# Two graph layers in one kernel: the first output bias moved from GpSimd to VectorE, loads and first products reordered, and a new order of work in the last slot

## The chip, the cores and the metric

The kernel runs on one core of one Trainium2 chip. The metric is the device time in microseconds (us) of one execution; the median of three runs of the kernel before is 3541.62 us (3541.19 to 3541.74). All numbers are float32.

Engine names are those of the profile: PE is TensorE (PEld its weight loads), DVE is VectorE, ACT is ScalarE, POOL is GpSimd, SP is SyncE, whose queue (SPq) issues all DMAs here.

## The reference, cut to what matters

There are 32 graphs of 512 nodes with 512 features. Layer 0 is attention with eight heads, weighted by the adjacency matrix, with an output projection, a residual and a layer norm. Layer 1 is a graph attention whose logits are a sum of one number per row and one per column.

```python
# layer 0, per graph
q = x @ Wq.T + bq;  k = x @ Wk.T + bk;  v = x @ Wv.T + bv      # 8 heads of 64
logits = q k^T / 8 + log(clip(adj, 1e-8))
out = softmax(logits) @ v
x = layer_norm(x + out @ Wo.T + bo) * gamma + beta
# layer 1, per graph
f = x @ fc_w.T + fc_b
masked = (f @ q_w.T + q_b) + (f @ k_w.T + k_b)^T + (1 - adj) * -1e9
out = softmax(leaky_relu(masked, 0.01)) @ f + x
```

## The kernel before, in words

**Slots.** The work is one stream, ordered by hand. For each graph ("batch") b of 32 there are four slots p, one for each pair of heads. A slot computes four score tiles (`score`, L754, 128 keys x 2 heads x 512 queries), takes their exponential on ScalarE (L759), multiplies them by the clipped adjacency on VectorE (`factors`, L767, from the tile `cT`), adds them up for the softmax's denominator (`sums`, L777 and L780) and multiplies them with v (`values`, L792). Between these, each slot carries pieces of other batches: projections of the next pair or the next batch (`seven_qk`, `seven_v`, seven products of half size in place of eight, with sums of their operands made on VectorE in `differences`, L560 to L563), the output projection of the batch before (`seven_wo`), its layer norm (`stats_units`, `normalise_units`) and the second layer of the batches before (`dots`, `softmax`, `eT`, `z`, `out_units`). The engines take their instructions in the order written; an instruction waits only for what it reads and for buffers to come free.

**Buffers.** PSUM has three pools: `ps_s` (two tiles of two banks: scores), `ps_o` (one bank: attention times v) and `ps_m` (three banks, used in turn by everything else). In SBUF the tiles `xT`, `n`, `yb` and `T` have a single buffer each.

**Head.** All loads are issued on SP, in program order: x of batch 0 in four pieces, then `load_first_constants` (L150: wq in four pieces, bq, wk in four pieces, bk, wv in one), sixteen loads of 64 KB for `cT` (L483, elements of 128 bytes), then the other constants. PE transposes x (L526), makes q and k of the first pair (L303) and two of the four 128-row units of v (`first_v[:2]`); then the slots begin. The other two units run inside slot (0, 0).

**Constants folded on the chip.** `fold_units` gives three functions that the slots of batches 0 and 1 call. `bias` (slot (0, 1)) adds bv times Wo to bo (L237, L238) and makes eight dot products of fc's rows with q_w and k_w (L241). `offset` (slot (0, 2)) makes the second layer's constant row and folds gamma (L247 to L259). `spread` (slot (1, 0)) sums two vectors over the partitions with a product into `ps_parts` (L273), read by a reduction on VectorE (L274), and broadcasts two more with the products `ps_uq` and `ps_uk` (L267, copied by L268).

**The bias of batch 0.** From batch 1 on, the projected output gets its bias by seeding a PSUM bank with it (`seed` in `seven_wo`, L704). For batch 0, `add_bo` (L281) adds it to the tile `n` on GpSimd with twelve adds of 128x256. The call is in `load_again` at the head of slot (1, 1); POOL has nothing else to do and runs it as soon as the bias is there.

**Denominators.** `divide` writes the sums to DRAM and back in another layout, `divided` (L828 to L838) inverts them there and brings them back as `R`, and `scale` (L847) multiplies.

**The last slot.** `last_slot` is written apart, for batch 31 (b) and the second layer of batch 30 (last). In order:

```python
here2[2]()                        # denominators of pair 2 of batch 31, VectorE (L886 to L892)
here3[2]()                        # the same of pair 3
zs = z(last); zs[0]()             # first of four z products (L439), ScalarE copies it to zT (L440)
wos = seven_wo(b, other_banks(b)); run(wos[:3])   # seed, products 1 2, 5 6
...                               # residual of batch 30 (L432, L433), products 3 7 and 4
run(stats_units(S[b], small, b))  # mean and variance of batch 31 (L330, L331)
run(zs[1:])                       # the other three z products
norm[0](); mask(S[b]); run(norm[1:])   # Ln, Exp (L349, L350), factors (L351 to L355), scaled rows (L359)
```

After that come batch 31's dot products (L369), the row of k values through DRAM to all partitions (`k_rows`, L386 and L388), batch 30's output (`out_units`, `pg`, L452, L453), batch 31's second softmax (L408 to L420), its transposes on PE (`pt_e`, L296), four z products, and four output products (`pg`), each followed by an addition on VectorE (L452) and a store of 128 rows (L453). `find_range` (L918 to L935) turns a record of all denominators into a flag: small operations on VectorE, a PE transpose `pf` (L926), a minimum (L927), a second transpose `one` (L931). The flag decides whether a general path is run afterwards; with these inputs it is not.

Of the kernel before, what the change touches and what calls it, by code (L numbers as in the profile page):

```python
# [19 lines left out]
P = 128  # L20
# [10 lines left out]
def kernel(  # L31
# [118 lines left out]
    def load_first_constants():  # L150
        K["wq"] = load_weight(wqT, "wq", 4)
        K["bq"] = load_col(const, bq, "bq")
        K["wk"] = load_weight(wkT, "wk", 4)
        K["bk"] = load_col(const, bk, "bk")
        K["wv"] = load_weight(wvT, "wv")
# [49 lines left out]
    def fold_units(psum, scratch):  # L205
# [57 lines left out]
        def spread():  # L263
            def copy(vector):
                _, _, _, dg, name, _ = vector
                ps = psum.tile([P, D], FP, tag="m", name=f"ps_{name}")
                nc.tensor.matmul(ps, ones, dg, start=True, stop=True)  # L267
                nc.vector.tensor_copy(K[name], ps)  # L268

            ps = psum.tile([P, D], FP, tag="m", name="ps_parts")  # L270
            for i, (_, _, part, _, _, b0) in enumerate(vectors):
                cols = ps[:, ts(i, DC)]
                nc.tensor.matmul(cols, ones, part, start=True, stop=True)  # L273
                nc.vector.tensor_reduce(extra[:, 0:1], cols, AX.X, ALU.add)  # L274
                nc.vector.tensor_add(b0, b0, extra[:, 0:1])
            for vector in vectors:
                copy(vector)
# [3 lines left out]
    def add_bo(n):  # L281
        left, step = (K["bo"][:, ts(h, H)] for h in range(2))
        for c in range(NC):
            nc.gpsimd.tensor_add(n[:, c, :H], n[:, c, :H], left)
            nc.gpsimd.tensor_add(n[:, c, H:], n[:, c, H:], left)
            nc.gpsimd.tensor_add(n[:, c, H:], n[:, c, H:], step)
# [156 lines left out]
    def out_units(s, dst, psum, name):  # L443
        ps = {}

        def mul(c):
            ps[c] = psum.tile([P, D], FP, tag="m", name=f"pg_{name}_{c}")
            product(ps[c], lambda i: s["zT"][:, i, ts(c, P)], lambda i: K["fc"][:, i, :])

        def add(c):  # L450
            o = s["yb"][:, c, :]
            nc.vector.scalar_tensor_tensor(o, ps[c], s["r"][:, c : c + 1], o, ALU.mult, ALU.add)  # L452
            nc.sync.dma_start(out=dst[ts(c, P), :], in_=o)  # L453
        return [(lambda c=c: mul(c), lambda c=c: add(c)) for c in range(NC)]


    def fast(ctx):
# [31 lines left out]
        def load_again(b):  # L489
# [7 lines left out]
            else:  # L497
                add_bo(s["n"])
# [175 lines left out]
        def seven_wo(b, banks):  # L674
# [53 lines left out]
            def unit3():  # L728
                mul(4, ps["a"], False)
                nc.vector.tensor_add(n21, ps["a"], n21)  # L730
# [180 lines left out]
        def find_range():  # L911
# [4 lines left out]
            def over_elements():  # L916
# [7 lines left out]
                nc.vector.tensor_reduce(low[:, 1:2], t, AX.X, ALU.min)  # L924
                pf = ps_m.tile([P, 512], FP, tag="m", name="pf")
# [11 lines left out]
            return over_elements, over_partitions  # L937
# [33 lines left out]
        def slot(b, p):  # L971
# [12 lines left out]
            run(values(b, p - 1) if p > 0 else values(last, 3) if last >= 0 else [])  # L984
# [30 lines left out]
            if p == 0:  # L1015
# [15 lines left out]
                run(units[2:])  # L1031
                if b == 0:
# [63 lines left out]
        def last_slot():  # L1096
# [31 lines left out]
            here2[2]()  # L1128
            here3[2]()
# [3 lines left out]
            wos = seven_wo(b, other_banks(b))  # L1133
            run(wos[:3])
# [9 lines left out]
            run(zs[1:])  # L1144
# [3 lines left out]
            run(norm[1:])  # L1148
            ks, qs = dots(b)
            run(ks)  # L1150
            k_rows(b)
            run(qs)
            outs = out_units(S[last], out[last], ps_m, last)
# [12 lines left out]
            range_steps = find_range()  # L1166
            range_steps[0]()
            zs[1]()
            flag = range_steps[1]()
            run(zs[2:])  # L1170
            run_out(out_units(S[b], out[b], ps_m, b))
# [8 lines left out]
        run(qk(0, 0) + first_v[:2])  # L1180
# [159 lines left out]
```

## Time and profile before

| what | value |
|---|---|
| median of 3 runs | 3541.62 us |
| profiled execution | 3541.68 us, its span 3539.9 us |
| PE busy | 3507.0 us, 99% of the span |
| DVE busy | 2741.2 us, 77% |
| ACT busy | 1305.9 us, 37% |
| POOL busy | 15.9 us, of which the twelve adds of `add_bo` run from 61.77 to 76.9 |
| mean granted clock of PE | 0.997 of full speed |
| HBM traffic | 61 GB/s over the span |

The profiled execution's own time is 1.8 us longer than the span that its trace covers. A line of a timeline reads: start, length (both us from the span's start), engine, line of the kernel, operation, output <- inputs, shapes, number of instructions merged; the bracket gives the idle time of the engine before it and what ended that. A merged row of several instructions gives their busy time from the first start to the last end. A row of the waits gives the total in us, how often, and the longest. The products are of float32 and each `matmul` of the program stands as two MATMUL instructions in the trace (four products of 128x512 make x8).

### The profile page before, as it was taken

What the parts mean: (1) busy time and instruction counts of PE and PEld (TensorE: products, weight loads), DVE (VectorE), ACT (ScalarE), POOL (GpSimd) and SP (SyncE); (2) the same over time, 40 slices, a digit from 0 to 9 for tenths busy, and PEclk for the clock granted to TensorE, in tenths of its full rate; (3) what the DMA queues carried; (4) which work ended last, traced back from release to release, by engine and by line L of the source; (5) the groups of instructions that cost most, each with busy time, mean ns of one, the idle gap of its engine ahead of it and who ended that gap; (6) DMA issues with size and microseconds to landing.
All of it is one profiled execution on the core that took longest, in us unless ns stands there. A gap on an engine that the chain in (4) does not pass through costs nothing.

```text
span 3539.9 us, 38498 instructions
## 1 busy us (share of the span) xinstructions
PE 3507.0 (99%) x13826; PEld 2045.0 (58%) x13826; DVE 2741.2 (77%) x4685; ACT 1305.9 (37%) x2120; POOL 15.9 (0%) x21
## 2 busy tenths in 40 slices
PE   9999999999999999999999999999999999999998
PEld 3555655655556656555556565565555665655554
DVE  6788877788787788777877877777778778787785
ACT  3334333333334343333333343333334333433442
POOL 1000000000000000000000000000000000000000
PEclk9999999999999999999999999999999999999999
DMA  4344233443233442334432334323344333443220
GB/s 113 49 75 87 46 74 65 77 87 58 70 73 62 87 81 52 75 60 81 87 56 68 71 66 87 69 64 75 61 81 87 52 69 68 72 87 63 68 77 28
DMA packets 880367, 250.68 MB, mean 71 GB/s; under 512 B 807212, under 2 KB 807212, under 8 KB 880168
## 3 DMA queue, kind: packets, MB, share of 16 engines
q1 hardware_dynamic: 880168, 248.15, 35.4%
q8 instruction: 110, 1.80, 0.2%
q14 instruction: 89, 0.73, 0.1%
HBM read 181.93 MB, written 34.65 MB: 61 GB/s over the span
## 4 chain that ended last, share of the span: by engine, by line
PE 96%; DVE 3%; DMA 1%; issue 0%; ACT 0%; SPq 0%; DVEq 0%; ACTq 0%
PE f L579 19%; PE sc L754 13%; PE po L792 13%; PE pz L303 12%; PE pg L303 12%; PE pw_a L199 7%; PE pv_a L199 5%; PE pw_c L199 3%; PE pv_b L199 3%; PE pv_c L199 3%; PE pq L579 2%; PE ps L809 2%; PE pw_b L199 2%; DVE at L767 1%; PE pv L303 0%
## 5 line engine op out<-in xcount | busy, mean ns | idle before, releaser
L759 ACT ACTIVATE at<-sc 128x1024 f32<-128x1024 f32 x512 | 496.4, 1021 | 788.7 <-PE sc L754 787.4
L767 DVE SCALAR_TENSOR_TENSOR at<-cT,at 128x1024 f32<-128x1024 f32 x512 | 603.8, 1221 | 173.3 <-ACT at L759 173.1
L754 PE MATMUL sc<-qT,kT 64*128 64x512 f32 x2048 | 508.9, 615 | 0.8 <-DVE qT L603 0.5
L792 PE MATMUL po<-at,v 128*64 128x512 f32 x2048 | 468.0, 599 | 0.0
L303 PE MATMUL pg<-fc,zT 128*128 128x512 f32 x1024 | 445.5, 593 | 0.2 <-DVE yb L452 0.2
L303 PE MATMUL pz<-eT,n 128*128 128x512 f32 x1024 | 445.5, 593 | 0.0
L754 PEld LDWEIGHTS sc<-qT,kT 64*128 64x128 f32 x2048 | 176.3, 186 | 297.1 <-issue 267.8
L303 PEld LDWEIGHTS pg<-fc,zT 128*128 128x128 f32 x1024 | 194.5, 190 | 233.1 <-issue 216.5
L303 PEld LDWEIGHTS pz<-eT,n 128*128 128x128 f32 x1024 | 194.7, 190 | 230.4 <-issue 220.8
L792 PEld LDWEIGHTS po<-at,v 128*64 128x64 f32 x2048 | 135.6, 137 | 316.5 <-issue 312.8
L780 DVE TENSOR_TENSOR as<-as,at 128x1024 f32<-128x1024 f32 x254 | 308.4, 1214 | 5.5
L579 PE MATMUL f<-T,qk_s 128*128 128x256 f32 x992 | 246.4, 381 | 8.5 <-DVE qT L588 4.3
L440 ACT COPY zT<-pz 128x512 f32<-128x512 f32 x128 | 74.9, 585 | 435.4 <-PE pz L303 435.4
L579 PEld LDWEIGHTS f<-T,qk_s 128*128 128x128 f32 x992 | 185.8, 191 | 38.7 <-DVE qT L588 5.1
L579 PE MATMUL f<-xT,wq 128*128 128x256 f32 x744 | 191.8, 380 | 0.0
L800 ACT COPY oT<-po 128x512 f32<-128x512 f32 x128 | 75.1, 587 | 288.1 <-PE po L792 288.1
L777 DVE TENSOR_TENSOR as<-at,at 128x1024 f32<-128x1024 f32 x128 | 154.2, 1204 | 2.2
L579 PEld LDWEIGHTS f<-xT,wq 128*128 128x128 f32 x744 | 139.0, 191 | 22.4
L591 ACT ACTIVATE qT<-f,bq 128x256 f32<-128x256 f32 x124 | 58.7, 473 | 234.9 <-PE f L579 234.9
L579 PE MATMUL f<-xT,qk_s 128*128 128x256 f32 x496 | 128.6, 382 | 0.0
L579 PE MATMUL f<-T,wk 128*128 128x256 f32 x496 | 127.3, 379 | 0.0
L579 PE MATMUL f<-xT,wk 128*128 128x256 f32 x496 | 127.3, 379 | 0.0
(204 smaller groups left out, 4582.6 us busy)
## 6 DMA issues: line engine op xcount, KB each, us to landing
cT<-in_adj_dram SPq DMA_DIRECT2D x512, 64.0 KB
out_dram<-yb SPq DMA_DIRECT2D x128, 256.0 KB
R<-d SPq DMA_DIRECT2D x126, 256.0 KB
x<-in_x_dram SPq DMA_DIRECT2D x124, 256.0 KB
e<-in_adj_dram SPq DMA_DIRECT2D x31, 1024.0 KB
n<-in_x_dram SPq DMA_DIRECT2D x31, 1024.0 KB
eP<-e SPq DMA_DIRECT2D x480, 64.0 KB
w<-dk SPq DMA_DIRECT2D x32, 256.0 KB
```

The lines of the kernel that those rows point to most:

```text
L199: nc.tensor.matmul(to[:, n, :], data(i, c)[:, ts(n, P)], weights[i][:, c, :], start=(first and n == 0 and c == 0), stop=(n == KH - 1 and c ...
L303: nc.tensor.matmul(ps, lhs(i), rhs(i), start=(i == 0), stop=(i == 3))
L440: nc.scalar.copy(s["zT"][:, d, :], pz)
L579: nc.tensor.matmul(to, left[i][:, c, ts(p, P)], s["B"][i][:, c, :], start=(first and c == 0), stop=(c == KH - 1), skip_group_check=True,)
L754: nc.tensor.matmul(sc[:, j, :], s["kT", p][rows, ts(kc, P)], s["qT", p][rows, :], start=True, stop=True,)
L759: nc.scalar.activation(at, sc, AF.Exp, scale=SCALE)
L767: nc.vector.scalar_tensor_tensor(at, cT[:, kc, :].unsqueeze(1).to_broadcast([P, 2, N]), ADJ_MIN, at, ALU.max, ALU.mult,)
L777: nc.vector.tensor_add(s["as", p], s["at", p, 0], s["at", p, 1])
L780: nc.vector.tensor_add(s["as", p], s["as", p], s["at", p, kc])
L792: nc.tensor.matmul(s["po", p][j * DK : (j + 1) * DK, :], s["v"][h // 4][:, kc, ts(h % 4, DK)], s["at", p, kc][:, j, :], start=(kc == 0), s ...
L800: nc.scalar.copy(s["oT"][p], s["po", p])
L809: nc.tensor.matmul(ps[h * BL : (h + 1) * BL, :], ones[:, :BL], s["as", p + h // 2][:, h % 2, :], start=True, stop=True,)
```

## The change

There are six parts.

1. Loads: bq and bk are loaded before wq, and wk is loaded as one DMA of 1 MB instead of four of 256 KB.
2. First products: only the first unit of v runs ahead of slot (0, 0); the second runs between that slot's first and second pair of score tiles.
3. `add_bo` runs on VectorE, with three adds of 128x1024 that broadcast the bias over the four row blocks, called at the end of slot (1, 0).
4. `spread` makes `uq` and `uk` first, and `ps_parts` after them.
5. The last slot: the seeds of `seven_wo` come ahead of pair 3's division and of the first zT copy; product 4 of `seven_wo` goes into a bank of its own and is added apart; the layer norm's operations on ScalarE come after the second z product and so ahead of the zT copies of the third and fourth; `find_range`'s small operations on VectorE come right after the dot products of q, and only its PE part stays among the z products.
6. The last output block is computed, added and stored in two halves of 256 columns.

```diff
--- before.py
+++ after.py
@@ -148,10 +148,10 @@
     K = {}
 
     def load_first_constants():
+        K["bq"] = load_col(const, bq, "bq")
+        K["bk"] = load_col(const, bk, "bk")
         K["wq"] = load_weight(wqT, "wq", 4)
-        K["bq"] = load_col(const, bq, "bq")
-        K["wk"] = load_weight(wkT, "wk", 4)
-        K["bk"] = load_col(const, bk, "bk")
+        K["wk"] = load_weight(wkT, "wk")
         K["wv"] = load_weight(wvT, "wv")
 
     def load_constants():
@@ -267,23 +267,24 @@
                 nc.tensor.matmul(ps, ones, dg, start=True, stop=True)
                 nc.vector.tensor_copy(K[name], ps)
 
+            for vector in vectors:
+                copy(vector)
             ps = psum.tile([P, D], FP, tag="m", name="ps_parts")
             for i, (_, _, part, _, _, b0) in enumerate(vectors):
                 cols = ps[:, ts(i, DC)]
                 nc.tensor.matmul(cols, ones, part, start=True, stop=True)
                 nc.vector.tensor_reduce(extra[:, 0:1], cols, AX.X, ALU.add)
                 nc.vector.tensor_add(b0, b0, extra[:, 0:1])
-            for vector in vectors:
-                copy(vector)
 
         return [bias, offset, spread]
 
     def add_bo(n):
-        left, step = (K["bo"][:, ts(h, H)] for h in range(2))
-        for c in range(NC):
-            nc.gpsimd.tensor_add(n[:, c, :H], n[:, c, :H], left)
-            nc.gpsimd.tensor_add(n[:, c, H:], n[:, c, H:], left)
-            nc.gpsimd.tensor_add(n[:, c, H:], n[:, c, H:], step)
+        left, step = (
+            K["bo"][:, ts(h, H)].unsqueeze(1).to_broadcast([P, NC, H]) for h in range(2)
+        )
+        nc.vector.tensor_add(n[:, :, :H], n[:, :, :H], left)
+        nc.vector.tensor_add(n[:, :, H:], n[:, :, H:], left)
+        nc.vector.tensor_add(n[:, :, H:], n[:, :, H:], step)
 
 
     def transpose_units(src, dst, psum, evict, name):
@@ -440,18 +441,27 @@
             nc.scalar.copy(s["zT"][:, d, :], pz)
         return [lambda d=d: unit(d) for d in range(DC)]
 
-    def out_units(s, dst, psum, name):
+    def out_units(s, dst, psum, name, halve=False):
+
         ps = {}
 
-        def mul(c):
-            ps[c] = psum.tile([P, D], FP, tag="m", name=f"pg_{name}_{c}")
-            product(ps[c], lambda i: s["zT"][:, i, ts(c, P)], lambda i: K["fc"][:, i, :])
-
-        def add(c):
-            o = s["yb"][:, c, :]
-            nc.vector.scalar_tensor_tensor(o, ps[c], s["r"][:, c : c + 1], o, ALU.mult, ALU.add)
-            nc.sync.dma_start(out=dst[ts(c, P), :], in_=o)
-        return [(lambda c=c: mul(c), lambda c=c: add(c)) for c in range(NC)]
+        def mul(c, cols):
+            ps[c, cols.start] = psum.tile(
+                [P, cols.stop - cols.start], FP, tag="m", name=f"pg_{name}_{c}_{cols.start}"
+            )
+            product(ps[c, cols.start], lambda i: s["zT"][:, i, ts(c, P)],
+                    lambda i: K["fc"][:, i, cols])
+
+        def add(c, cols):
+            o = s["yb"][:, c, cols]
+            nc.vector.scalar_tensor_tensor(
+                o, ps[c, cols.start], s["r"][:, c : c + 1], o, ALU.mult, ALU.add
+            )
+            nc.sync.dma_start(out=dst[ts(c, P), cols], in_=o)
+        parts = [(c, slice(0, D)) for c in range(NC)]
+        if halve:
+            parts[-1:] = [(NC - 1, slice(h * H, (h + 1) * H)) for h in range(2)]
+        return [(lambda a=a: mul(*a), lambda a=a: add(*a)) for a in parts]
 
 
     def fast(ctx):
@@ -494,8 +504,6 @@
                 s["n"] = act.tile([P, NC, D], FP, tag="n", name=f"n_{b}")
             if b > 0:
                 load_b(s["n"], x[b])
-            else:
-                add_bo(s["n"])
             if b < B - 1:
                 s["e"] = act.tile([P, NC, N], FP, tag="L1", name=f"e_{b}", bufs=2)
                 load_b(s["e"], adj[b])
@@ -671,7 +679,7 @@
                 nc.vector.tensor_add(c21, ps["a"], c21)
             return [unit0, unit1, unit2, unit3]
 
-        def seven_wo(b, banks):
+        def seven_wo(b, banks, apart=False):
 
 
 
@@ -726,8 +734,13 @@
                 nc.vector.tensor_add(n22, ps["a"], n22)
 
             def unit3():
-                mul(4, ps["a"], False)
-                nc.vector.tensor_add(n21, ps["a"], n21)
+                if apart:
+                    mul(4, ps["b"], True)
+                    nc.vector.tensor_add(n21, ps["a"], n21)
+                    nc.vector.tensor_add(n21, ps["b"], n21)
+                else:
+                    mul(4, ps["a"], False)
+                    nc.vector.tensor_add(n21, ps["a"], n21)
             return [seed, unit0, unit1, unit2, unit3]
 
         def long_banks(b):
@@ -922,6 +935,8 @@
                 nc.vector.tensor_mul(t, t, t)
                 nc.vector.tensor_scalar(t, t, 0.25, None, ALU.is_le)
                 nc.vector.tensor_reduce(low[:, 1:2], t, AX.X, ALU.min)
+
+            def turn():
                 pf = ps_m.tile([P, 512], FP, tag="m", name="pf")
                 nc.tensor.transpose(pf[:2, :P], low, ident)
                 nc.vector.tensor_reduce(least, pf[:2, :P], AX.X, ALU.min)
@@ -934,7 +949,7 @@
                 flag = const.tile([1, 1], I32, name="flag")
                 nc.vector.tensor_scalar(flag, bad, -1.0, 1.0, ALU.mult, ALU.add)
                 return flag
-            return over_elements, over_partitions
+            return over_elements, turn, over_partitions
 
         def work(b):
             S[b]["w"] = io.tile([P, 4, N], FP, tag="x", name=f"w_{b}")
@@ -981,7 +996,7 @@
             if p == 1 and last >= 0:
                 wos = seven_wo(last, long_banks(last))
                 run(wos[:1])
-            run(values(b, p - 1) if p > 0 else values(last, 3) if last >= 0 else [])
+            run(values(b, p - 1) if p > 0 else values(last, 3) if last >= 0 else first_v[1:2])
             if p == 0 and last >= 0:
                 scale(last, 0)
                 first_difference(last)
@@ -1029,6 +1044,8 @@
                 if b == 1 and nxt < B:
                     load_x(nxt)
                 run(units[2:])
+                if b == 1:
+                    add_bo(S[0]["n"])
                 if b == 0:
                     run(combine(K["wv"], K["v_s"])[1:])
                 if b >= 2:
@@ -1126,12 +1143,13 @@
             for u in here3[:2]:
                 u()
             here2[2]()
+            wos = seven_wo(b, other_banks(b), apart=True)
+            wos[0]()
             here3[2]()
             zs = z(last)
             zs[0]()
             first_sum(b)
-            wos = seven_wo(b, other_banks(b))
-            run(wos[:3])
+            run(wos[1:3])
             new_yb(last)
             residual(S[last], slice(0, 1))
             residual(S[last], slice(1, 2))
@@ -1141,15 +1159,18 @@
             wos[4]()
             invert(S[last])
             run(stats_units(S[b], small, b))
-            run(zs[1:])
+            zs[1]()
             norm = normalise_units(S[b], small, b)
             norm[0]()
             mask(S[b])
             run(norm[1:])
+            run(zs[2:])
             ks, qs = dots(b)
             run(ks)
             k_rows(b)
             run(qs)
+            range_steps = find_range()
+            range_steps[0]()
             outs = out_units(S[last], out[last], ps_m, last)
             soft = softmax(b)
             run_out(outs[:1])
@@ -1163,12 +1184,11 @@
             rest_of_layer1(b)
             zs = z(b)
             run(eT(b) + zs[:1])
-            range_steps = find_range()
-            range_steps[0]()
+            range_steps[1]()
             zs[1]()
-            flag = range_steps[1]()
+            flag = range_steps[2]()
             run(zs[2:])
-            run_out(out_units(S[b], out[b], ps_m, b))
+            run_out(out_units(S[b], out[b], ps_m, b, True))
             return flag
 
         load_x(0)
@@ -1177,7 +1197,7 @@
         load_constants()
         first_xT()
         first_v = v(0)
-        run(qk(0, 0) + first_v[:2])
+        run(qk(0, 0) + first_v[:1])
         turn_a(range(NC))
         bias, offset, spread = fold_units(
             ps_m,
```

## The prediction

> **What bounds the kernel now.** I read the page's table of busy times first, then PE's waits in the first 210 us and in the last 100 us, then the timelines around each of those waits.
>
> ```profile
> PE 3507.0 (99%) x13826; PEld 2045.0 (58%) x13826; DVE 2741.2 (77%) x4685; ACT 1305.9 (37%) x2120; POOL 15.9 (0%) x21
> ```
>
> TensorE is idle for 3539.9 - 3507.0 = 32.9 us only. The table of stretches has PE busy for 3170.00 of the 3170 us from 230 to 3400, and the diff touches nothing that runs there. So the time can move only in the first two batches and in the last slot. PE's waits there (us in total, times, longest), first 0 to 210, then 3440 to 3540:
>
> ```profile
> PE f L579 <- DVE qT L588: 4.3, 2, 2.4
> PE f L579 <- DVE T L560: 4.2, 2, 2.7
> PE ps_parts L273 <- DVE fold_more L274: 2.8, 1, 2.8
> PE pv L303 <- DMA wv<-in_wvT_dram: 2.1, 1, 2.1
> PE sc L754 <- ACT at L759: 0.3, 1, 0.3
> ```
> ```profile
> PE pt_e L296 <- ACT cT L420: 4.7, 4, 4.0
> PE pf L926 <- DVE low L924: 1.6, 1, 1.6
> PE pw_a L199 <- DVE n L726: 1.2, 1, 1.2
> PE pw_a L199 <- ACT pw_a L704: 1.2, 1, 1.2
> PE pg L303 <- DVE yb L452: 0.2, 1, 0.2
> ```
>
> A wait costs more than its length. In the table of stretches (length, busy of PE, PEld, DVE, ACT and POOL, granted clock, DMA) the clock falls after the longer ones:
>
> ```profile
> 94.00:98.00 4.00, 3.52 (x9) 2.87 (x10) 3.93 (x6) 0.47 (x1) 0.00 (x0) 0.57 0.32 86
> 132.00:136.00 4.00, 4.00 (x9) 1.23 (x10) 1.46 (x4) 0.00 (x0) 0.00 (x0) 0.57 0.00 0
> 3498.00:3502.00 4.00, 2.08 (x6) 1.20 (x7) 3.46 (x6) 3.07 (x9) 0.00 (x0) 0.50 0.25 98
> ```
>
> The waits of 2.67 us (at 94.48), 1.86 (104.31), 2.80 (131.65), 2.41 (198.88) and 4.03 (3499.23) are each followed by such a stretch; those of 1.2 and 1.6 us are not. Price of one: from 94.48 to 98.83 PE issues 12 matmuls of 128x256 that take 2.69 us elsewhere (0.97 + 0.86 + 0.86 at 123.35 to 125.97), so 1.66 us are lost.
>
> **The Trainium skill.** "TensorE: Matmul & The Clock Gate", What's actually happening: an idle stretch of about one free-running 3.4 us window halves PE's clock. The trace agrees on the half and on some 3.4 us, but 1.86 us of idleness were enough. "SBUF — State Buffer", Who interferes with whom: a VectorE instruction with two SBUF inputs contends with a GpSimd instruction that reads SBUF. The trace agrees: while POOL runs L284 to L286 (61.77 to 76.9), the start-to-start of L241 is 1.14 us, against 0.73 for the same form at L369 (3487.66 to 3490.44), and L767 takes 6.74 us for four, against 4.63 at 27.05.
>
> ```profile
> 61.77 0.96 POOL L284 TENSOR_TENSOR n<-n,bo 128x256 f32<-128x256 f32 x1 [60.26 <-DVE bo L237]
> 64.47 1.10 DVE L241 SCALAR_TENSOR_TENSOR fold_rows<-fc,fold_rows 128x512 f32<-128x512 f32 x1
> 71.20 6.74 DVE L767 SCALAR_TENSOR_TENSOR at<-cT,at 128x1024 f32<-128x1024 f32 x4
> ```
>
> **Part by part.**
>
> *Loads.* bq and bk (2 KB each) move ahead of wq; wk becomes one DMA, so SP issues 12 DMAs up to wv instead of 15. Each SP issue takes 0.3 to 0.6 us, so wq goes out some 1 us later (3.6 instead of 2.60); wv, which now waits at 8.74 for a piece of wq to land, goes out around 6.8 (estimate: after x's fourth piece, which PE has consumed by 7.84), and the 16 cT loads behind it as much earlier. But the stream is limited by transfer: 4.09 MB of the 4.19 MB of x, wq, wk and wv have moved by 14.0 (288 to 396 GB/s from 2 to 14), and wv's last part lands at 8.74 + 8.90 = 17.64. The same bytes stand ahead of wv, so I take 0; bounds -2.1 (the whole wait) and +1.0 (wk complete only after its 1 MB; PE now starts it at 12.04). The wait hides up to 2.1 us of a late wk.
>
> *First products.* v's second unit (8 matmuls, 3.44 us) moves between the first and second pair of scores: no work changes, and the wait of 0.27 for ScalarE goes. VectorE still cannot start L767 before cT's last transpose ends (25.9). -0.3.
>
> *First bias.* Off POOL: twelve adds. VectorE's eight L241 shrink by 8 x 0.4 = 3.2 us, its four L767 by 2.1, together 5.3. Next late: L510 overwrites xT while PE reads it until 76.28, and L247 needs ps_bfc, which ends at 79.81; so L247 starts at 79.95 instead of 84.02, 4.1 us sooner, and from there VectorE runs without a gap to L588 (103.84). L560 then ends at 90.3, ahead of PE's need at 91.81: its wait of 2.67 and its slow clock (1.66) go, 4.3. But L588 moves by 4.1 only and PE by 4.3, so the next wait stays, 1.86 + 0.2, with its slow clock. Sum -4.1; bounds -5.8 (no slow clock there) and -2.5.
>
> On VectorE: three adds of 128x1024 with a broadcast row, not in this trace; nearest rows L780 (1.214) and half of L432's 2.29, so 3.5 to 3.7 us. They stand after `divided` in batch 1's first slot, ahead of L767, with R's DMAs already issued. VectorE idles there 0.85 (before 137.67) and 1.94 (before 143.23, for R), and the reordering below gains it the rest. I take 0; if the cover fails, L861 is late for pw_b and PE pays up to 3.6.
>
> *Spread reordered.* Now PE does a ps_parts product, waits for L274 (behind VectorE's work until 131.44), then uq and uk. After: uq, uk (1.72 us at full clock) and one ps_parts run from 128.56 to 130.4; L274 comes behind two copies (131.44 + 2 x 0.61), so PE resumes at 132.85. With the last product the scores start at 133.0 instead of 133.6 (the order of before at full clock). -0.6, the slow clock kept, because 2.4 us of idleness remain; bounds -2.3 and +0.2.
>
> *Last slot.* (a) Seeds: ScalarE's two L704 copies no longer stand behind the zT copy; PE's 1.17 goes. Next late: oT of pair 3 (L892 ends at 3458.4), needed by the second product: 0.6 comes back. (b) Product 4 into its own bank: the 1.18 behind L726 goes; VectorE adds once more (0.61), and pz2 gets that bank around 3471.8, when PE wants it. PE starts pz1 about 2.1 us sooner. (c) Statistics: Ln stands behind three zT copies that PE paces.
>
> ```profile
> 3481.54 0.30 ACT L349 ACTIVATE rstd<-mv,eps 128x4 f32<-128x4 f32 x1
> 3482.11 0.16 DVE L351 TENSOR_TENSOR rt<-rstd 128x4 f32<-128x4 f32 x1 [6.92 <-ACT rstd L350]
> 3493.11 1.33 ACT L408 ACTIVATE w<-w,q 128x512 f32<-128x512 f32 x2 [7.08 <-DMA w<-dk]
> 3499.23 0.48 PE L296 MATMUL pt_e<-ident,cT 128*128 128x128 f32 x1 [4.03 <-ACT cT L420]
> ```
>
> After, it starts when the statistics end (3475.1): 6.4 sooner, and with it dots, k's four DMAs, w's DMA, logits, exponentials and transposes. The two zT copies moved behind L359 (2.93 us, then 0.58 each) end at 3480.1 and 3480.7; PE's pg needs them at 3480.5 and 3481.3: covered by 0.4. The out3 store moves along, so L432 does too. PE finishes pg3 2.4 sooner, so the wait for exponentials shrinks from 4.7 to about 2. (d) The six small range operations (1.1 us) move into VectorE's idle time ahead of L409 (2.42): pf's 1.61 goes. Chain 6.4 + 1.6 = 8.0, the slow clock kept; up to 9.5 without it. Bounds -5 (zT copies late) and -9.5.
>
> *Halves.* The last L452 on 128x256 like L603: 0.42 instead of 0.75. The store of 128 KB isn't in the trace: from its issue at 3534.92 to the span's end 5.0 us pass for 256 KB; the gain lies between 0 and 0.9, I take 0.4. The 16 matmuls of half width take 16 x 0.216 (eight take 1.73, 98.83 to 100.56) = 3.45, as the 8 full ones. The first half's store (0.33 issue) lies 1.7 us ahead. -0.7.
>
> Sum: 0.3 + 4.1 + 0.6 + 8.0 + 0.7 = 13.7. The profiled run took 3541.68 (span 3539.9 and 1.8 around it), 0.06 over the median, so 3541.62 - 13.7 = 3527.9; as of three slow-clock stretches one may well vanish, I say 3527.
>
> **Rivals.** A, the sum: 3521 to 3530, by how many slow stretches vanish; 0.72. B, the bias takes VectorE's slack in batch 1: 3527.9 + 3.6 = 3531.5; for it, VectorE is busy from 114.7 to 137 with little idle time, against it the 2.8 us of idle time behind; 0.13. C, PE waits for zT behind L359, because mv comes later than 3475: half the chain's gain goes, 3532; 0.08. D, the reordering does nothing net: VectorE-bound waits reappear one step on and the chain keeps 2 us: 3538; 0.04. E, slower: wk in one piece, wv and cT share the engines so that wk completes with everything queued. PE would start pk late; each us beyond 14 is paid in full. It decides from a first v product later than 17.8 + 13.7 = 31.5; if wk takes until 36, with v's product 3.44 behind, the time is 3527.9 + 21.6 = 3549.5. Against it, even the last cT piece was transposed by 25.9; 0.03.
>
> A measurement of this kernel can tell about 0.2% (7 us) from no change: faster 0.93, same 0.04, slower 0.03. The range reaches from A's best to C: 3520.5 to 3532.
>
> **What would show it.** L241 at 0.69 and no POOL adds; no PE wait for T L560 in batch 0 but one for qT L588 of about 2; ps_uq near 128 with ps_parts behind; Ln six us ahead of the last zT copies' end; pf without a wait. Wrong if PE waits at pw_b for oT L847, at pg for zT, or for wk.

## The result: 3524.22 us, 0.45% faster

The changed kernel takes 3524.22 us (median of 5 runs, 3524.01 to 3527.14), the kernel before 3541.19 in the same series (3539.29 to 3541.74). The ratio is 0.9955 with a 95% interval of 0.9940 to 0.9969. The forecast was 3527 (3520.5 to 3532). The profiled execution of the changed kernel is the slowest of the five (3527.14, span 3525.4), so the traces account for 14.5 us of the 17.0 between the medians. The changed kernel was timed in this series only. In the later series, on other chips, the kernel before took 3539.94, 3538.90 and 3539.97; across series, compare ratios and stretches of the traces, not times.

The busy times of the profile after (per engine: us, share of the span, instructions):

```profile
PE 3503.8 (99%) x13834; PEld 2041.8 (58%) x13834; DVE 2739.6 (78%) x4690; ACT 1305.6 (37%) x2120; POOL 0.9 (0%) x9
```

PE's idle time went from 32.9 to 3525.4 - 3503.8 = 21.6 us, and it is busy for 3.2 us less although it has eight matmuls more. Most of that is slow clock that went. A *window* here is 3.41 us long, the shortest time for which the records show the clock at half; a *slow stretch* is one window or two. Up to PE's last product the profile before has six such windows and the one after four. PE's waits, first 0 to 212, then 3420 to 3540 (us in total, times, longest; the wait for x at the start, 3.6 us, and two rows of 0.5 or less are left out):

```profile
PE f L587 <- DVE qT L596: 4.8, 2, 2.4
PE pk L304 <- DMA wk<-in_wkT_dram: 1.9, 1, 1.9
PE ps_parts L275 <- DVE fold_more L276: 1.9, 1, 1.9
PE f L587 <- DVE T L568: 1.6, 1, 1.6
```
```profile
PE pt_e L297 <- ACT cT L421: 1.6, 4, 0.4
PE pw_b L199 <- DVE oT L905: 0.6, 1, 0.6
```

Gone are the wait for T in batch 0 (that of batch 1 is left), for wv, for both causes at pw_a, for pf and most of that for the exponentials. New are the waits for wk and at pw_b. Cut at landmarks that both traces have, the span divides as follows. (A landmark is the start of a PE row in the timeline; the third score of a slot is the first after its first pair.)

| stretch | before, us | after, us | difference | forecast |
|---|---|---|---|---|
| start to the first score of slot (0, 1) | 42.97 | 43.54 | +0.57 | -0.3 |
| from there to the first score of slot (1, 0) | 71.00 | 65.29 | -5.71 | -4.1 |
| to the third score of slot (1, 1) | 26.97 | 27.83 | +0.86 | -0.6 |
| to the first z product of batch 30 | 3311.11 | 3311.09 | -0.02 | 0 |
| to the end of PE's last product | 82.05 | 72.89 | -9.16 | -8.0 |
| to the end of the span | 5.80 | 4.76 | -1.04 | -0.7 |

The 3311 us in between moved by 0.02.

### The profile page after: what moved, and what is told of

Read it like the earlier page. It is cut to its first block, busy times and chain, and to the rows that moved or that the text cites. A ratio compares the mean times of both kernels' runs of the same rounds, so it can differ in the third digit from the quotient of the medians.

```text
span 3525.4 us, 38493 instructions
## 1 busy us (share of the span) xinstructions
PE 3503.8 (99%) x13834; PEld 2041.8 (58%) x13834; DVE 2739.6 (78%) x4690; ACT 1305.6 (37%) x2120; POOL 0.9 (0%) x9
## 4 chain that ended last, share of the span: by engine, by line
PE 96%; DVE 2%; issue 0%; DMA 0%; ACT 0%; SPq 0%; DVEq 0%; ACTq 0%
PE f L587 19%; PE sc L767 14%; PE po L805 13%; PE pg L304 12%; PE pz L304 12%; PE pw_a L199 6%; PE pv_a L199 5%; PE pw_c L199 3%; PE pv_b L199 3%; PE pv_c L199 3%; PE pq L587 2%; PE ps L822 2%; PE pw_b L199 2%; PE pk L304 0%; PE pv L304 0%; DVE at L780 0%
## 5 line engine op out<-in xcount | busy, mean ns | idle before, releaser
L780 DVE SCALAR_TENSOR_TENSOR at<-cT,at 128x1024 f32<-128x1024 f32 x512 | 601.7, 1217 | 175.2 <-ACT at L772 175.0
L304 PE MATMUL pg<-fc,zT 128*128 128x512 f32 (+1 forms) x1032 | 445.3, 589 | 0.0
```

Source lines behind the costliest of these rows:

```text
L304: nc.tensor.matmul(ps, lhs(i), rhs(i), start=(i == 0), stop=(i == 3))
L780: nc.vector.scalar_tensor_tensor(at, cT[:, kc, :].unsqueeze(1).to_broadcast([P, 2, N]), ADJ_MIN, at, ALU.max, ALU.mult,)
```

## The experiments

Five to eight runs of one kernel scatter by 2.4 to 5.9 us (the 21 of `e2_bias_only` by 5.3), so what a small edit does is read from the stretches in its trace; a time settles only differences above some 3 us. Each kernel has one trace. Ratios are to the kernel before in the same series, with 95% intervals. In the diffs, `...` stands for lines left out.

### POOL's reads and VectorE

`e2_bias_only`, the kernel before with the new `add_bo` and its new place:

```diff
-            else:
-                add_bo(s["n"])
...
+                if b == 1:
+                    add_bo(S[0]["n"])
```

> The kernel before with only the first bias moved to VectorE. Theory 1 (taking POOL's reads away speeds VectorE, and the adds hide in its idle time): L241 at 0.69, no wait for L560 in batch 0, slot (1, 0) begins 4.1 to 5.8 us sooner, and of this all is kept at slot (2, 0): 3536 to 3537. Rival (VectorE's 3.6 us of new adds are paid in batch 1): slot (1, 0) sooner by as much, but slot (2, 0) by 2 us or less: 3539.

It took 3535.41 us, ratio 0.9986 (0.9980 to 0.9993), 4.5 us under the 3539.94 of the kernel before in that series and a little under the range of theory 1. From slot (0, 1) to slot (1, 0) the stretch is 66.80 us against 71.00 (with the slow clock behind the wait for qT, as before), and from there to the third score of slot (1, 1) 26.90 against 26.97: the new adds cost PE nothing there, against rival B of the forecast.

`e8_pool_busy`, the changed kernel with POOL work of the old size put back, on a tile that is idle:

```diff
                     bias()
+                    for i in range(6):
+                        t = S[0]["n"][:, i % 4, ts(i // 4, H)]
+                        nc.gpsimd.tensor_add(t, t, K["bo"][:, :H])
+                        nc.gpsimd.tensor_sub(t, t, K["bo"][:, :H])
```

> The changed kernel, with twelve adds on POOL of the size of the old ones at their old time, added and subtracted again on a tile that nobody needs then. Theory 1 (the contention of POOL with VectorE cost the time): L241 back to about 1.1 and four L780 to about 6.7 us, PE waits for L568 again in batch 0, slot (1, 0) 4 to 6 us later than in the changed kernel: 3528 to 3530. Rival (what helped was only that the work left its place, or the order around it): L241 stays at 0.69 and the time at 3524.

It took 3530.45 us (ratio 0.9973, 0.9963 to 0.9984), by the ratios some 6 us more than the changed kernel. The row of the eight dot products (duration in ns: least, median, most), first in the changed kernel, then here:

```profile
L241 DVE SCALAR_TENSOR_TENSOR fold_rows<-fc,fold_rows x8: 685/691/692, 62.6 to 67.8; 128x512 f32<-128x512 f32 x8
```
```profile
L241 DVE SCALAR_TENSOR_TENSOR fold_rows<-fc,fold_rows x8: 1090/1095/1219, 62.9 to 71.0; 128x512 f32<-128x512 f32 x8
```

And PE's two longest waits in all of this kernel from 0 to 212 us, but for x:

```profile
PE f L587 <- DVE qT L596: 4.3, 2, 2.4
PE f L587 <- DVE T L568: 4.2, 2, 2.7
```

Twelve POOL instructions for whose results nobody waits bring back 0.40 us on each of eight VectorE instructions and, some 25 us later, PE's wait for T, 2.65 us in batch 0 where before had 2.67. The four L780 take 6.74 us again, the number of before. From slot (0, 1) to (1, 0) the stretch is 70.97 us, the 71.00 of before. So it was POOL's work at the same time, and not its place in the order.

### The order of `spread`

`e4_spread_old`, the changed kernel with the old order:

```diff
-            for vector in vectors:
-                copy(vector)
             ps = psum.tile([P, D], FP, tag="m", name="ps_parts")
...
+            for vector in vectors:
+                copy(vector)
```

> The changed kernel with ps_parts ahead of uq and uk again. Theory 1 (the reordering only moves PE's wait behind uq and uk; it gains less than 1 us and what decides is how long the slow clock lasts behind it): the wait of 2.8 us returns, with the time of the head within 2 us of the changed kernel's, 3522.5 to 3526. Rival (the reordering gives 2 us or more, as the shorter wait would say): 3526.5 or more.

3526.59 us (3522.80 to 3527.22), just on the rival's side of the line, ratio 0.9962 (0.9948 to 0.9975), which overlaps that of the changed kernel: the time doesn't decide. The stretch from the first score of slot (1, 0) to the third of slot (1, 1) says more. With the old order it is 26.90 to 26.97 us in four traces (before, `e1_tail_only`, `e2_bias_only`, this one), each with the slow clock behind the wait of 2.8. With the new order it is 24.7 us in three traces (`e5_stats_late`, `e7_wk_pieces`, `e9_range_late`), where no slow clock followed, and 26.3 to 27.9 in four (`e10_no_halves`, the changed kernel, `e8_pool_busy`, `e3_loads_old`), where one did. The mean of the seven is 26.3: a gain of 0.7, with a spread of 3.2 that the order doesn't control. The changed kernel's own profile has one of the longest; its table of stretches shows the clock (third number from the end):

```profile
128.00:132.00 4.00, 4.00 (x12) 1.45 (x11) 3.53 (x9) 1.02 (x1) 0.00 (x0) 0.50 0.02 2
132.00:136.00 4.00, 4.00 (x16) 1.27 (x16) 3.97 (x4) 1.02 (x1) 0.00 (x0) 0.72 1.01 194
```

The traces also show what decides whether a slow stretch follows: how the wait falls on the windows. In every trace the slow stretches begin a whole number of windows of 3.413 us after the first record of the clock and after each other (before: 94.50, 104.75, 132.05 and 200.32, which are 3, 8 and 20 windows apart). Cut along these windows, the same wait for qT of 2.41 us looks like this in the changed kernel and in `e3_loads_old` (after the length comes PE's busy time):

```profile
96.71:100.12 3.41, 1.74 (x9) 1.18 (x7) 3.41 (x4) 1.17 (x2) 0.00 (x0) 1.00 0.71 110
100.12:103.53 3.41, 2.67 (x12) 2.39 (x13) 1.11 (x3) 0.47 (x1) 0.00 (x0) 1.00 0.70 111
```
```profile
98.87:102.28 3.41, 1.14 (x5) 1.03 (x6) 2.22 (x4) 0.49 (x1) 0.00 (x0) 1.00 0.73 115
102.28:105.69 3.41, 3.41 (x9) 2.72 (x9) 0.42 (x1) 0.47 (x1) 0.00 (x0) 0.50 0.52 83
```

In the first, the wait is split and no window has more than 1.67 us without PE; in the second, one window has 2.27, and the next is at half clock. The wait for qT of 2.41 us occurs 23 times in batches 0 and 1 of all traces. In 14 cases a window held 1.98 us or more of idleness, and a slow stretch followed each; in 9 no window held more than 1.93, and none followed. Of the seven traces with the new order, the four with a slow stretch behind `ps_parts` have 1.74 to 2.02 us in one window, the other three 1.14 to 1.43. The four traces with the old order, whose wait is 2.80 us, have 2.28 to 2.80. So the line lies between 1.74 and 1.98 us in the first 212 us. On which side a wait of some 2 us falls depends on where it meets the windows; what the order of `spread` changes is the length, so that a split can be enough to avoid the slow stretch. (Among the short transposes of the last slot the clock also fell behind windows with 1.45 to 1.54 us; the count holds for the head.)

`e6_parts_together`, both products into ps_parts first, their reductions behind the copies:

```diff
+            for i, (_, _, part, _, _, _) in enumerate(vectors):
+                nc.tensor.matmul(ps[:, ts(i, DC)], ones, part, start=True, stop=True)
             for vector in vectors:
                 copy(vector)
...
-                nc.tensor.matmul(cols, ones, part, start=True, stop=True)
```

> The changed kernel with both ps_parts products one after the other, ahead of uq and uk, and their two reductions on VectorE behind the copies. Theory 1 (PE waits there only because the second product into the tile stands behind the first one's reduction): no PE wait for the reduction, no slow clock in slot (1, 1), and from the first score of slot (1, 0) to the third of slot (1, 1) 27.8 - 1.9 - 2.9 = 23 us; time 3519 to 3522. Rival (VectorE is behind and the wait comes back at the scores or at the output projection): 26 us or more, and 3524.

The stretch is 23.18 us, as expected, without a slow clock. The wait is not all gone: two of 0.56 us are left (for VectorE's additions of qT, which hold the bank for `ps_uk`, and at pw_b for L860, the second behind the stretch). The time, 3523.60 (ratio 0.9958, 0.9944 to 0.9971), is above what was expected. The expectation had taken 4.8 us, read from the changed kernel's profile of 3527.14, off its median of 3524.2. Profile against profile, 3.5 us are gained: 4.65 in the stretch, of which 1.1 come back right behind it (slot (1, 2) begins 21.56 us after the third score of slot (1, 1), 20.43 in the changed kernel), in part because PE now comes early enough to wait for L860, which stands behind the new adds. The table of stretches of this kernel for the first of the two rows above:

```profile
128.00:132.00 4.00, 4.00 (x20) 1.33 (x20) 3.90 (x8) 1.50 (x3) 0.00 (x0) 1.00 0.13 25
```

`e12_filler`, two products into a free bank, to keep PE busy where it waits:

```diff
                 nc.tensor.matmul(cols, ones, part, start=True, stop=True)
+                if i == 0:
+                    spare = K["ps_o"].tile([P, N], FP, tag="po", name="spare")
+                    for _ in range(2):
+                        nc.tensor.matmul(spare, ones, K["wq"][:, 0, :], start=True, stop=True)
```

> The changed kernel with two products of 128x512 into a PSUM bank that is free, put between the two ps_parts products, where PE waits 1.9 us: their results go nowhere. Theory 1 (PE's idleness there causes the slow clock behind it): the second ps_parts product starts no later, the granted clock stays at 1.00 from there to 136, and the stretch of 27.8 us takes 25; time 1 to 3 us less than the changed kernel. Rival (the clock falls for another reason, power or the phase of the program): the clock falls as before and the time is the same or 0.5 us more.

No slow clock followed, and the stretch took 24.70 us; the time was 3524.56 (ratio 0.9959, 0.9945 to 0.9972). Three kernels without the filler have 24.7 as well, where the wait was split between two windows. One trace can't tell the filler from such a split: whether it gains anything isn't shown.

### The loads

`e7_wk_pieces`:

```diff
-        K["wk"] = load_weight(wkT, "wk")
+        K["wk"] = load_weight(wkT, "wk", 4)
```

> The changed kernel with wk in four pieces again, but bq and bk still ahead of wq. Theory 1 (the single piece makes PE wait for the whole 1 MB, 1.2 to 2.2 us, and now and then its clock falls behind that): no wait for wk above 0.5 us, slot (0, 1) begins at 41.5 to 42.5 instead of 43.5; time 1 to 2 us less. Rival (the stream of bytes decides and what pk no longer waits, v's first product waits for wv): slot (0, 1) begins at 43 or later; the same time.

`e3_loads_old`, the loads of the first constants as before:

```diff
-        K["bq"] = load_col(const, bq, "bq")
-        K["bk"] = load_col(const, bk, "bk")
         K["wq"] = load_weight(wqT, "wq", 4)
-        K["wk"] = load_weight(wkT, "wk")
+        K["bq"] = load_col(const, bq, "bq")
+        K["wk"] = load_weight(wkT, "wk", 4)
+        K["bk"] = load_col(const, bk, "bk")
```

> The changed kernel with the load order of the kernel before, but with v's first unit alone ahead of slot (0, 0). Theory 1 (the stream of bytes decides when wv is there, the order of the small loads does nothing): no wait for wk, a wait for wv of 0.8 to 2.2 us, slot (0, 1) at 40.5 to 42.7. Rival (bq and bk in front save a us or more): slot (0, 1) at 42.7 or later.

With pieces, PE starts pk at 11.40 in `e7_wk_pieces`, waits 0.86 for wv, and slot (0, 1) begins at 40.86, the earliest of all traces. But `e11_best` below has the same loads and begins it at 42.03. With the whole piece it begins at 41.3 to 42.3 where no slow clock followed the wait for wk (`e12_filler`, `e4_spread_old`, `e10_no_halves`, `e5_stats_late`, `e9_range_late`) and at 43.3 to 43.8 where one did (changed kernel, `e6_parts_together`, `e8_pool_busy`). The times don't tell the loads apart (`e7_wk_pieces` 3524.76, ratio 0.9961, 0.9948 to 0.9975). `e3_loads_old` has no wait for wk and only 0.57 for wv, yet its slot (0, 1) begins at 43.83, which is the rival's number but not for the rival's reason. The products of q and k in it and in `e7_wk_pieces`:

```profile
8.78 6.04 PE L304 MATMUL pq<-xT,wq 128*128 128x512 f32 x8
14.66 3.60 PE L304 MATMUL pk<-xT,wk 128*128 128x512 f32 x8
```
```profile
7.86 3.70 PE L304 MATMUL pq<-xT,wq 128*128 128x512 f32 x8
11.40 3.60 PE L304 MATMUL pk<-xT,wk 128*128 128x512 f32 x8
```

The same eight products take 6.04 us in one and 3.70 in the other, with no wait between them. The records of the granted clock tell why, although they begin late (the tables of stretches print 1.00 where there is no record yet). Their first entry, at full clock, stands at 13.53 us in `e3_loads_old` and at 7.83 in `e7_wk_pieces`. If PE runs at half clock until that entry, the eight products take 3.67 us, as in `e6_parts_together` where it stands ahead of them, plus half the time from their start to the entry: 3.67 + (13.53 - 8.78) / 2 = 6.05 for `e3_loads_old`. The sum meets the measured time of all 14 traces within 0.03 us, except the changed kernel's (0.11; its products also wait 0.2 for wq).

This also says when the single piece costs time. Where the first entry comes before 8 us, PE is through with q early. Then the whole piece made it wait 1.92 to 2.15 us, each time with a slow stretch behind (changed kernel, `e6_parts_together`, `e8_pool_busy`), and slot (0, 1) began 2.4 to 3.0 us later than with pieces (`e7_wk_pieces`, one trace). Where it comes after 11.6 us, the whole piece is there in time, and slot (0, 1) begins at 41.82 and 42.27 (`e10_no_halves`, `e9_range_late`) against 42.03 with pieces (`e11_best`). Whether the order of bq and bk matters stays open; 3525.85 us (ratio 0.9960, 0.9946 to 0.9973) doesn't say either.

### The last slot

`e1_tail_only`, the kernel before with the edits of the last slot alone (the lines of `out_units` and `seven_wo` are those of the change):

```diff
+            wos = seven_wo(b, other_banks(b), apart=True)
+            wos[0]()
...
-            run(zs[1:])
+            zs[1]()
...
             run(norm[1:])
+            run(zs[2:])
...
+            range_steps = find_range()
+            range_steps[0]()
...
-            range_steps = find_range()
-            range_steps[0]()
+            range_steps[1]()
...
-            run_out(out_units(S[b], out[b], ps_m, b))
+            run_out(out_units(S[b], out[b], ps_m, b, True))
```

> The kernel before with only the last slot's edits and the output in halves. Theory 1 (two separate gains: about 9.2 us in the last slot plus 1.0 behind the last product, and about 4.3 in the head): 3541.2 - 10.2 = 3531.0, with the first score of slot (2, 0) at 208.5 as before. Rival (the last slot's gain depends on the head, for instance through the phase of PE's clock): less than 8 us of gain in the last slot.

3529.92 us, ratio 0.9972 (0.9961 to 0.9984), 10.0 under before. From the first z product of batch 30 to PE's last product it takes 72.96 us, as in the changed kernel (72.89). The last slot gains as much with the old head as with the new one, against the rival. The ratios of this kernel and of `e2_bias_only` are 0.28% and 0.14% under 1, together 0.42% of the 0.45% of the whole change.

`e5_stats_late`:

```diff
-            zs[1]()
+            run(zs[1:])
             norm = normalise_units(S[b], small, b)
...
-            run(zs[2:])
```

> The changed kernel with the layer norm's ScalarE work behind all zT copies again. Theory 1 (the early statistics give most of the last slot's gain: the chain over dots, k's row, logits and exponentials starts 6.4 us sooner): the wait for exponentials before pt_e returns to 4 to 7 us, and from the first z product of batch 30 to the span's end 6 to 8 us are lost: 3530 to 3532. Rival (seeds, the bank of its own and the range operations give most): 2 us or less lost.

3528.61 us, ratio 0.9971 (0.9960 to 0.9982): 4.4 over the changed kernel (5.7 by the ratios), less than expected. The stretch to PE's last product is 78.88 us (72.89 + 6.0), the lower end of theory 1. The wait for the exponentials is longer again, 3.12 us for the first, though under the 4 to 7 expected. Of the 6.0 us some 2.8 are slow clock behind it (estimate: half of the 5.5 us that PE is busy in the two slow windows from 3487.68 to 3494.51):

```profile
3481.49 3.70 PE L304 MATMUL pg<-fc,zT 128*128 128x512 f32 x8 [1.19 <-DVE yb L457]
3488.30 0.48 PE L297 MATMUL pt_e<-ident,cT 128*128 128x128 f32 x1 [3.12 <-ACT cT L421]
3490.42 3.03 PE L297 MATMUL pt_e<-ident,cT 128*128 128x128 f32 x13 [0.23 <-ACT cT L421]
```

In the changed kernel the thirteen transposes behind the last exponential take 1.66 us, at full clock:

```profile
3490.99 1.66 PE L297 MATMUL pt_e<-ident,cT 128*128 128x128 f32 x13 [0.38 <-ACT cT L421]
```

`e9_range_late`:

```diff
-            range_steps = find_range()
-            range_steps[0]()
             outs = out_units(S[last], out[last], ps_m, last)
...
             run(eT(b) + zs[:1])
+            range_steps = find_range()
+            range_steps[0]()
             range_steps[1]()
```

> The changed kernel with the six small range operations on VectorE back among the z products. Theory 1 (they stand behind the residual's two passes, which wait for the output store, while PE is now sooner): pf waits for L937 for about 3 us, more than the 1.6 of the kernel before, and the time is 2 to 5 us more than the changed kernel's 3524. Rival (the wait shrinks as the whole chain moves): 1.6 us or less.

3526.30 us (ratio 0.9965, 0.9953 to 0.9977), within theory 1's range; the wait is 1.48 us, the rival's. In this trace the z product ahead of pf ran partly at half clock (4.54 us for eight, instead of 3.6 to 3.7) and covered 0.9 us of it; even so the wait would stay under the 3 us expected. The stretch is 76.25 us; the three traces with one slow window there, too, and the range early have 74.3 to 74.4 (`e7_wk_pieces`, `e12_filler`, `e11_best`), so the range operations are worth 1.8 us.

`e10_no_halves`, the last output in one piece:

```diff
-            run_out(out_units(S[b], out[b], ps_m, b, True))
+            run_out(out_units(S[b], out[b], ps_m, b))
```

> The changed kernel with the last output block in one piece. Theory 1 (a shorter last addition and a smaller last store): from PE's last product to the span's end 5.8 us as before, against 4.8; the time 0.5 to 1.5 us more. Rival (the end is a fixed cost): the same 4.8.

From PE's last product to the end 5.1 us, time 3524.64 (ratio 0.9957, 0.9944 to 0.9971). In the eleven traces with halves that end takes 4.7 to 5.6 us, mean 5.0; in the three with one piece (before, `e2_bias_only`, this) 5.8, 6.1 and 5.1, mean 5.7. A gain of 0.7 is possible, but it lies within the scatter and isn't shown.

### A version that goes further

`e11_best` puts wk in pieces and the ps_parts products together as above, and moves one VectorE addition in slot 3 of batches 0 and 1:

```diff
-            if p % 2:
+            if p % 2 and (p == 1 or b > 1):
                 sums(b, p, 0)
...
                 turn_a((0, 1))
+                if b < 2:
+                    sums(b, p, 0)
                 sums(b, p, 1)
```

> The changed kernel with three things together: wk in four pieces, both ps_parts products one after the other, and in slot 3 of batches 0 and 1 the first sum of the softmax's denominator (1.2 us on VectorE) moved behind the projections' additions. Theory 1 (each PE wait in batches 0 and 1 is VectorE's order): the two waits for qT of 2.4 us shrink to 1.2 or less, slot (2, 0) begins 4 to 5 us before that of the kernel with the wk pieces (198.4), and fewer slow stretches follow: 3515 to 3520. Rival (the deferred sum makes something else late, as the score tiles' buffers): a wait in slot (1, 0) or (2, 0), and 3523 or more.

3520.49 us, ratio 0.9944 (0.9930 to 0.9958), the lowest of all, just above the range expected; its interval overlaps that of the changed kernel. Both waits for qT are 1.15 us instead of 2.41, and no slow stretch is recorded in the head. PE's waits of 1 us and more there, but for x:

```profile
PE f L587 <- DVE qT L596: 2.3, 2, 1.2
PE f L587 <- DVE T L568: 1.6, 1, 1.6
PE ps_uk L267 <- DVE qT L596: 1.0, 1, 1.0
```

Slot (2, 0) begins at 196.27, 2.1 sooner than with the pieces alone (198.39), not the expected 4 to 5, because its slot (0, 1) began 1.2 later (42.03) and a wait of 1.05 for `ps_uk` came in.

## Why the forecast was right, and where its steps were not

**Place and sum.** That only head and last slot can move held to 0.02 us in 3311. The sum of 13.7 us met the 14.5 of the profiles in part by luck: the table's differences from the forecast are +0.87, -1.61, +1.46, -0.02, -1.16 and -0.34 us and partly cancel; the large ones are mostly slow stretches that came (loads, `spread`) or stayed away (bias, last slot). The forecast's list of waits with a slow clock behind them left one out that says so: PE's wait for wv in the kernel before, 2.15 us from 15.63 on, with no slow stretch until 94.50. Whether one follows wasn't set by the length alone.

**Bias.** The mechanism held in each step: L241 at 0.69, four L780 in 4.63, L568 ahead of PE's need, three adds of 1.16 to 1.23 us ahead of L780 in batch 1 and no PE wait for them:

```profile
68.38 4.63 DVE L780 SCALAR_TENSOR_TENSOR at<-cT,at 128x1024 f32<-128x1024 f32 x4
129.20 1.16 DVE L285 TENSOR_TENSOR n<-n,bo 128x1024 f32<-128x1024 f32 x1
130.27 1.21 DVE L286 TENSOR_TENSOR n<-n,bo 128x1024 f32<-128x1024 f32 x1
131.52 1.23 DVE L287 TENSOR_TENSOR n<-n,bo 128x1024 f32<-128x1024 f32 x1
```

The wait for qT stayed, 2.41 instead of the 2.1 worked out. The size, -5.71 against -4.1, differs by a slow stretch behind that wait: the forecast kept it, and this execution had none. Of the ten traces with this wait in batch 0 it came in four; `e2_bias_only` is one of them, with -4.20.

**Loads.** Here the step failed that took 0, with +1.0 as its bound. A PE wait for wk was one of the forecast's three signs of being wrong, and it came: wk arrives at 13.28, 1.9 us after PE wants it. wv is no longer waited for, so the wait moved from wv to wk; but the slow clock behind the moved wait was left out. pk takes 5.37 us instead of 3.60, and the first product of v starts 0.84 us later than before (18.62 against 17.78):

```profile
13.41 5.37 PE L304 MATMUL pk<-xT,wk 128*128 128x512 f32 x8 [1.92 <-DMA wk<-in_wkT_dram]
18.62 3.60 PE L304 MATMUL pv<-wv,xT 128*128 128x512 f32 x8
```

**First products.** Held: from the first product of v to slot (0, 1) it takes 24.92 us, 25.19 before, 0.27 less where 0.3 was said. No run changes this part alone.

**Spread.** The move of the wait behind uq and uk was right (1.87 us, 2.4 expected), the mean of seven traces gives -0.7 where -0.6 was said; the profiled execution gives +0.86, as its slow stretch lasted two windows (6.8 us) where the forecast kept one.

**Last slot.** The table's -9.16 lies near the -9.5 that the forecast gave for no slow clock, and there was none behind pt_e. In detail: the second z product of batch 30 (pz1) starts 16.47 us after the first (pz0) instead of 18.51, 2.0 sooner (2.1 said); the wait at pw_b is 0.58 (0.6); Ln starts 6.1 sooner, counted from pz0 (6.4). These lines of the changed kernel answer to those of before:

```profile
3471.14 0.30 ACT L350 ACTIVATE rstd<-mv,eps 128x4 f32<-128x4 f32 x1 [2.70 <-DVE mv L332]
3471.70 0.16 DVE L352 TENSOR_TENSOR rt<-rstd 128x4 f32<-128x4 f32 x1 [0.60 <-ACT rstd L351]
3482.75 1.34 ACT L409 ACTIVATE w<-w,q 128x512 f32<-128x512 f32 x2 [6.17 <-DMA w<-dk]
3488.87 0.33 PE L297 MATMUL pt_e<-ident,cT 128*128 128x128 f32 x1 [0.44 <-ACT cT L421]
```

Ln now waits for the statistics (2.70 us), no longer for PE's products. But the forecast gave the whole 6.4 to the order of the statistics. In `e5_stats_late` Ln stands 27.5 us behind pz0, against 29.5 before and 23.4 in the changed kernel: 2 of the 6 us come with the seeds and the bank, which start PE's z products sooner (by what is left over; no run has these two alone), and 4 from the order. The two gains aren't separate terms.

**Halves.** 0.7 said, 1.04 in this pair, 0.7 between the means, within the scatter.

**Rivals.** B fell with `e2_bias_only`; where PE runs ahead, it shows a little (0.56 us at pw_b in `e6_parts_together` and `e11_best`). C fell: the two zT copies behind L360 end at 3476.58, and PE doesn't wait at pg. D and E didn't come; wk's late arrival, E's mechanism, is there at 1.9 us of the 14 that it needed.

The forecast missed the median by 2.8 us. The profile is 2.9 us over that median, and its mean granted clock is 0.998 where the other four runs have 0.999; over the whole run a thousandth is some two windows, 1.7 us each when PE is busy in them. That fits slow stretches as the cause of the miss, but the other four runs have no trace, so it isn't shown. The Trainium skill, "TensorE: Matmul & The Clock Gate", What's actually happening, says that the window is free-running and doesn't begin anew with a kernel. The traces agree: the first record of the clock stands at 6.90 to 13.53 us, and the same wait of 2.41 us in batches 0 and 1 was followed by a slow stretch in 14 of 23 cases, that of 1.56 us in none of 14.

## What to carry to other kernels

- On a kernel whose main engine is 99% busy, look for its few waits outside the steady part, and price each with the clock behind it. A wait of 2.4 us was followed by a slow stretch of some 1.7 us more in 14 of 23 cases here, one of 1.15 us in neither of two; so shortening it can be worth more than the 1.25.
- An idle engine is not a free place for work: twelve GpSimd adds that nobody waited for slowed eight VectorE instructions with two inputs in SBUF by 0.4 us each, four larger ones by 0.5, and TensorE paid some 25 us later.
- In a tail of dependent small steps, check what stands ahead of each in its engine's queue; here a statistic that was ready waited behind copies that TensorE paced, and some 4 us went with it.

## What the hardware showed unexpectedly

- From the first record of the clock to 212 us, TensorE's clock fell to half behind every window of 3.413 us with 1.98 us or more of idleness and behind none with less than 1.74. It stayed there for one window mostly, for two in the changed kernel (127.43 to 134.26).
- The first eight 128x512 products took from 3.67 to 6.04 us, by the moment of the first record of full clock (6.90 to 13.53 us), so the head's length varies by some 2 us from one execution to the next before any edit.
